# A Mamba scan and a mixture of experts on one core: the end of the scan, the pairs' preparation, the scatters and the shared expert emitted in the order of a list schedule

## The chip, the cores and the metric

The program runs on one core of a Trainium2 chip. The metric is device microseconds (us) of one execution. The kernel is written for five engines that run side by side, each through its own queue in order: PE (TensorE, matmuls and transposes), DVE (VectorE), ACT (ScalarE), POOL (GpSimd, which here also issues the scatters) and SP (which issues most transfers). An instruction starts when it is at the head of its queue and what it waits for has arrived.

## The reference

Eight sequences of 512 tokens, 128 wide (in the kernel B = 8, and a sequence is NC = 4 chunks of Q = 128). First an attention-like part, four layers of a Mamba-2 scan, and then a mixture of experts, each inside a layer norm with shift, scale and gate.

```python
mod = (_silu(L0_c) @ L0_wmod).reshape(L0_c.shape[0], 6, 1, -1)
h = _layernorm(x, axis=-1) * (1 + ca) + sa
x = x + ga * _L0_attn_ref(h, ...)        # 4 layers, then a final rms norm
h = _layernorm(x, axis=-1) * (1 + cb) + sb
x = x + gb * _L0_ffn_ref(h, ...)

# one step of the scan, per sequence
hs = hs * dA_t[:, :, None, None] + dtx_t[..., None] * B_t[:, None, None, :]
y = jnp.einsum('bhpn,bn->bhp', hs, C_t)

# the experts
normed = hidden_states * rsqrt(mean(hidden_states ** 2) + 1e-08) * norm_weight
shared = jnp.maximum(normed @ sw1 + sb1, 0.0) @ sw2 + sb2
probs = jax.nn.sigmoid(flat @ router_w.T)
scores, idx = jax.lax.top_k(probs, TOPK)          # 2 of 8 experts for a token
w = scores / (jnp.sum(scores, axis=-1, keepdims=True) + 1e-06)
return shared + routed
```

## The kernel before

**The scan.** A unit is one sequence in one layer, U = 32 of them; an item is one chunk of a unit, NI = 128 of them, item i being chunk i % 4 of unit i // 4. The scan is computed chunk by chunk, with a state carried from chunk to chunk of a sequence. Items 96 to 111 are the last layer of sequences 0 to 3, items 112 to 127 that of sequences 4 to 7. A loop over slots t emits, in a fixed order, pieces of several items: the loads of decay rows of item t + 4 (`decay_rows`), the difference and the mask of the decays of t + 3 on POOL (`decay_diff`, `decay_mask`), their exponential of t + 2 on ACT (`decay_exp`), transposes of t + 2 on PE and their copy on ACT (`transposes`, which ends in the copy), weighing of t + 1 on POOL (`weigh`), the gram matrix of t + 1 on PE (`gram`), the mix of both on DVE (`mix`), the state's products and step (`state_out`, `state_decay` on POOL, `state_next` on DVE), the output of t - 1 (`chunk_out`, `gate`, `square`), its projection at t - 2 (`project_out`, `out_scale`, whose power is on POOL), and the addition to h at t - 3 (`out_add`). Each piece waits for the one before it of its item, and stands in its engine's queue behind the pieces of other items. From item 115 on, decays are worked at half width on POOL and ACT (`whole`). Units are prepared four units ahead (LEAD), so the last preparation is emitted up to slot t = 115, and from t = 112 on (`drain`) only items remain.

**The pairs.** Four sets of two sequences go through `rejoin(g)`: final rms norm (squares on ACT, power F), addition to x, layer norm (statistics on DVE, power L), shift and scale, rms norm (squares, power G), rows for the experts, transposes, router product, choice of two experts and their places (`first_largest`, prefix sums, the product `pos`), and 16 scatters of 128 rows each to the experts' lists in DRAM (`scatter`, `xg`). A set is called sorted when its row numbers `ix` are there. Powers are on POOL for sets 0 and 1 and on DVE, in twelve steps, for sets 2 and 3. `rejoin` is a generator; every slot steps each of them (`step_pairs`, and once more at its end), set g from slot t = 106 + 8 g on. In slots t >= 112 one scatter is emitted in each slot.

**The shared expert** (`shared`) makes for each sequence four products `phs` with the first weights, ReLU copies on ACT, sixteen products `pes` with the second, and a copy of the sum. It is stepped once a slot from t = 112 on, as soon as a sequence is routed.

**Behind the scan** a loop steps the pairs that are left, emits all scatters that are ready, steps the shared expert, and when the last set is counted, the `tables`: which expert and which rows each of the NT = 39 tiles of 256 rows has. Then come the weights of three tiles (`fetch`), their rows from `xg`, which wait for all scatters, and the experts: `turn`, `hidden`, `combine` for each tile, a scatter of the results to `yg`, and at the end two gathers and a sum per sequence.

**What sets the order.** Slots and the loop behind them are in a manual schedule: all engines follow the order in which the source emits. In the loop behind the scan POOL is left out of it, and the framework's scheduler chooses POOL's order. Three PSUM banks (`pbank`) go round among pairs and shared expert.

Of the kernel before, what the change touches and what calls it, by code (L numbers as in the profile page):

```python
# [20 lines left out]
LEAD = 4  # L21

# [14 lines left out]
def adaln_mamba_moe(  # L37
# [262 lines left out]
    hTx, scatters, rowpools, banks, held = {}, [], [frow], [], {}  # L300
    sets = [(b, b + 1) for b in range(0, B, 2)]
    routed = set()
    scratch = scb.rearrange("p b q -> p (b q)")
# [16 lines left out]

    def mean_squares(h, eps, name, on_pool):
        n = h.shape[1]
        ss = small.tile([P, G2], F32, tag="pss", name=f"pss{name}")[:, :n]
        for j in range(n):
            nc.scalar.activation(unread, h[:, j, :], AF.Square, accum_out=ss[:, j : j + 1])  # L325
            if j % NC == NC - 1:
                yield
        v = small.tile([P, G2], F32, tag="pv", name=f"pv{name}")[:, :n]
        nc.vector.tensor_scalar(v, ss, 1.0 / DM, eps, ALU.mult, ALU.add)
        return power(v, name, on_pool)  # L330

    def rejoin(g):


        seqs = sets[g]
        b0, n = seqs[0], len(seqs) * NC
        parts = [slice(i * NC, (i + 1) * NC) for i in range(len(seqs))]
        md = []
# [6 lines left out]
        def both(k):  # L345

            for i, t in enumerate(parts):
                yield t, md[i][:, k, :].unsqueeze(1).to_broadcast([P, NC, DM])

        mine = slice(b0 % 2 * NC, b0 % 2 * NC + n)  # L350
        h, xt = (v[b0 // 2].rearrange("p b s d -> p (b s) d")[:, mine] for v in (hp, xp))
        on_pool = g < 2
        rs = yield from mean_squares(h, 1e-5, f"F{g}", on_pool)
        yield
        for j in range(n):
            nc.scalar.activation(h[:, j, :], h[:, j, :], AF.Copy, scale=rs[:, j : j + 1])
            if j % NC == NC - 1:
                yield
        for t, m in both(0):
            nc.vector.tensor_mul(h[:, t, :], h[:, t, :], m)  # L360
        yield
        nc.vector.tensor_add(xt, xt, h)
        yield
        mv = small.tile([P, G2, 2], F32, tag="pmv", name=f"mvF{g}")[:, :n]
        for i in range(len(seqs)):
            st = small.tile([P, NC, 6], F32, tag="st", name=f"stF{g}_{i}")
            for s in range(NC):
                nc.vector.bn_stats(st[:, s, :], xt[:, i * NC + s, :])
            for s in range(NC):
                nc.vector.bn_aggr(mv[:, i * NC + s, :], st[:, s, :])  # L370
            yield
        v = small.tile([P, G2], F32, tag="pv", name=f"pvL{g}")[:, :n]
        nc.vector.tensor_scalar_add(v, mv[:, :, 1], 1e-5)
        rs = power(v, f"L{g}", on_pool)
        if on_pool:
            yield
        off = small.tile([P, G2], F32, tag="poff", name=f"off{g}")[:, :n]
        nc.vector.scalar_tensor_tensor(off, mv[:, :, 0], -1.0, rs, ALU.mult, ALU.mult)
        yield
        for j in range(n):  # L380
            nc.scalar.activation(
                h[:, j, :], xt[:, j, :], AF.Identity, bias=off[:, j : j + 1], scale=rs[:, j : j + 1]
            )
            if j % NC == NC - 1:
                yield
        for k in (2, 1):
            for t, m in both(k):
                nc.vector.tensor_tensor(h[:, t, :], h[:, t, :], m, ALU.mult if k == 2 else ALU.add)
            yield
        rs = yield from mean_squares(h, 1e-8, f"G{g}", on_pool)  # L390
        yield

        while scatters and scatters[0][0] in held.get(len(rowpools), [])[:-1]:
            yield
        held.setdefault(len(rowpools), []).append(g)
        rows = [rowpools[-1].tile([P, G2, RW], F32, tag=f"row{c}", name=f"row{c}_{g}")[:, :n] for c in range(2)]
        for j in range(n):
            nc.scalar.activation(rows[0][:, j, :DM], h[:, j, :], AF.Copy, scale=rs[:, j : j + 1])  # L398
            if j % NC == NC - 1:
                yield  # L400
        for c in range(2):
            nc.scalar.activation(rows[c][:, :, DM + 1], tok[:, :n], AF.Copy, bias=float(c * T + b0 * L))
        for i, b in enumerate(seqs):
            t = parts[i]
            pt = banks[-1](f"ptF{b}")
            for s in range(NC):
                nc.tensor.transpose(pt[:, s * P : (s + 1) * P], rows[0][:, i * NC + s, :DM], ident)
            nc.vector.tensor_copy(rows[1][:, t, :DM], rows[0][:, t, :DM])
            yield
            hTx[b] = h[:, t, :].rearrange("p s d -> p (s d)")  # L410
            nc.scalar.activation(hTx[b], pt[:, :L], AF.Copy, scale=nw)
        yield
# [9 lines left out]
        routed.update(seqs)  # L422
        yield
# [11 lines left out]
        m = n * E  # L435
        p = t3("prob")
        nc.scalar.activation(p.rearrange("p s e -> p (s e)"), pr[:, :m], AF.Exp, scale=-1.0)
        yield
# [13 lines left out]
        m1, oh1 = first_largest(p, 1)  # L452
        rest = t3("rest")
        nc.vector.scalar_tensor_tensor(rest, oh1, -2.0, p, ALU.mult, ALU.add)
        yield
        m2, oh2 = first_largest(rest, 2)

        mx, before = t3("mx"), t3("before")
        nc.vector.tensor_add(mx, oh1, oh2)
        yield  # L460
        while len(taken) <= g:
            yield

# [8 lines left out]
        before = src  # L472
        pp = banks[-1](f"pos{g}")
        nc.tensor.matmul(pp[:, :m], below, mx.rearrange("p s e -> p (s e)"), start=True, stop=False)
        nc.tensor.matmul(pp[:, :m], ones, before.rearrange("p s e -> p (s e)"), start=False, stop=True)
        taken.append(fp.tile([P, E], F32, name=f"taken{g + 1}"))
        nc.vector.tensor_add(taken[g + 1], before[:, n - 1, :], mx[:, n - 1, :])
# [3 lines left out]
        yield  # L481
# [6 lines left out]
        for c, oh in enumerate((oh1, oh2)):  # L488
            nc.vector.tensor_mul(oh, oh, pos)
            ix = rowpools[-1].tile([P, G2], mybir.dt.uint32, tag=f"ix{c}", name=f"ix{c}_{g}")[:, :n]  # L490
# [3 lines left out]
            for j in range(n):  # L494
                scatters.append((g, xg, rows[c][:, j, :], ix[:, j : j + 1], "rows"))
        yield
# [15 lines left out]
    xbp = front.enter_context(tc.tile_pool(name="xbp", bufs=5, side="right"))  # L512
# [15 lines left out]
    accs, w12, late = {}, [], []  # L528

    def evacuate(fn, n):  # L530

        if fn is not None:
            late.append(fn)
        while len(late) > n:
            late.pop(0)()

    def shared():

        hds = {}

        def relu(hd, k, ph):
            nc.scalar.activation(hd[:, k, :], ph[:, :L], AF.Relu, bias=b1[:, E, k : k + 1])  # L542

        def keep(b, pe):
            accs[b] = hp[b // 2][:, b % 2]
            nc.scalar.copy(accs[b].rearrange("p s d -> p (s d)"), pe)

        def second(b):
            hd = hds.pop(b)
            pe = pbank(f"pes{b}")  # L550
            for s in range(NC):
                for k in range(FK):
                    nc.tensor.matmul(  # L553
                        pe[:, s * DM : (s + 1) * DM],
# [5 lines left out]
                if s % 2 and s < NC - 1:  # L560
                    yield
            evacuate(lambda: keep(b, pe), 2)
            yield

        for b in range(B):
            while b not in routed:
                if hds:
                    evacuate(None, 0)
                    yield from second(b - 1)
                else:  # L570
                    yield
            hds[b] = hd = xbp.tile([P, NX, L], F32, tag="xbc", name=f"hds{b}")
            for k in range(FK):
                ph = pbank(f"phs{b}_{k}")
                nc.tensor.matmul(ph[:, :L], w12[0][:, k * P : (k + 1) * P], hTx[b], start=True, stop=True)  # L575
                evacuate(lambda hd=hd, k=k, ph=ph: relu(hd, k, ph), 2)
                yield
            if b - 1 in hds:
                yield from second(b - 1)
        evacuate(None, 0)  # L580
        yield from second(B - 1)
        evacuate(None, 0)

    serving = shared()

    def serve():
        nonlocal serving
        if not step(serving):
            serving = None

    with ExitStack() as actx:
# [18 lines left out]
        ss, rss, hns, last_po = {}, {}, {}, []  # L610
# [182 lines left out]
        def sums_b(g):  # L793
# [13 lines left out]
            if g >= (U - LEAD) // GROUP:  # L807
                ncum[g] = scratch[:, m * (g % 2) : m * (g % 2 + 1)]
# [67 lines left out]
        def transposes(i):  # L876
# [5 lines left out]
            for k in range(w // P):  # L882
                nc.tensor.transpose(pt[:, k * P : (k + 1) * P], xbc[u][:, k, t], ident)
# [543 lines left out]
```

## Time and profile before

| what | us |
|---|---|
| median of 9 runs | 1108.61 (1106.09 to 1110.78) |
| the profiled execution's own time | 1110.51 |
| its span | 1108.8 |
| experts, 940 to 1080: PE busy | 130.3 of 140 |
| last addition to h in the scan ends | at 839.96 |
| first scatter to xg starts | at 782.24 |
| last scatter to xg ends | at 916.66 |

Times in the span are counted from its start. The profile gives for each engine how long it was busy in a stretch, each instruction with its start and length, the idle time before it and what ended that, and the chain of waits followed back from the end. A line number there is one of the kernel before; L500 is the call in `scatter`, L310 and L313 to L318 are `power`, L1015 is the power in `out_scale`, L1023 is `out_add`, L907 is `mix`, L841 and L849 are `decay_diff` and `decay_mask`, L575 is the first product of the shared expert, L1271 the request for an expert's rows.

### The profile page before, as it was taken

To read this page: it belongs to the slowest core of one execution; us is meant where nothing else is said; L and a number is where in the kernel's file an instruction comes from. 1 tells how busy PE (TensorE), PEld (TensorE's weight loads), DVE (VectorE), ACT (ScalarE), POOL (GpSimd) and SP (SyncE) were. 2 spreads that over 40 slices of the span, in tenths; PEclk is the share of its full clock that TensorE was granted. 3 is DMA by queue.
4 is the path that set the end of the run, shared out by engine and by line. 5 is a ranking of instruction groups with operands and counts; after the bars stand their busy time and mean duration, and the time that the engine had idled before them with its cause. 6 is when DMAs were issued, how large, how long until landed. Compare 5 with 4: busy or idle time off the path is not lost. (4 is left out here: it accounts for less than half of the span.)

```text
span 1108.8 us, 21442 instructions
## 1 busy us (share of the span) xinstructions
PE 954.8 (86%) x7130; PEld 728.4 (66%) x7130; DVE 827.7 (75%) x1990; ACT 768.4 (69%) x1725; POOL 828.6 (75%) x841
## 2 busy tenths in 40 slices
PE   4568999999999999999999999867666957999985
PEld 2236677767777767777767776556554746888872
DVE  3667889889999898998989898867474464665653
ACT  4577998889889889889889888797535622333320
POOL 6867889889889999899899898775834463555550
PEclk9777999999999999999999999967867988999997
DMA  5141444546555546444334334243000035777747
GB/s 115 5 145 41 139 150 154 179 143 186 169 177 185 168 137 199 163 149 148 117 100 132 113 125 147 82 143 129 32 18 30 27 109 155 218 216 211 225 141 232
DMA packets 134301, 151.18 MB, mean 136 GB/s; under 512 B 22568, under 2 KB 106696, under 8 KB 134192
## 3 DMA queue, kind: packets, MB, share of 16 engines
q1 hardware_dynamic: 127184, 137.91, 41.3%
q0 software_dynamic: 4672, 9.42, 2.5%
q10 hardware_dynamic: 2336, 2.50, 0.7%
q8 instruction: 56, 0.92, 0.3%
q14 instruction: 53, 0.43, 0.1%
HBM read 120.07 MB, written 29.71 MB: 135 GB/s over the span
## 5 line engine op out<-in xcount | busy, mean ns | idle before, releaser
L698 DVE SCALAR_TENSOR_TENSOR xbc<-px,cw,xbc 128x511 f32<-128x511 f32 (+2 forms) x384 | 286.0, 745 | 30.8 <-ACT xbc L688 23.7
L841 POOL TENSOR_TENSOR dV<-dV,cum 128x1024 f32<-128x1024 f32 (+1 forms) x128 | 231.9, 1812 | 0.0
L907 DVE TENSOR_TENSOR dV<-dV,ptx 128x1024 f32<-128x1024 f32 x128 | 155.2, 1212 | 16.2 <-ACT xT L885 16.2
L849 POOL TENSOR_SCALAR_AFFINE_SELECT dV<-dV 128x1024 f32<-128x1024 f32 x128 | 141.8, 1108 | 9.3
L892 POOL TENSOR_TENSOR xd<-xT,dt 128x512 f32<-128x512 f32 (+1 forms) x128 | 120.6, 943 | 34.6 <-ACT xT L885 34.6
L500 POOL DMA_INDIRECT yg<-y,ix x78 | 84.2, 1079 | 81.0 <-DVE y L1313 66.3
L862 ACT ACTIVATE dV<-dV 128x1024 f32<-128x1024 f32 (+1 forms) x128 | 129.1, 1009 | 14.7 <-POOL dV L849 14.4
L688 ACT ACTIVATE xbc<-px,cbias,cw 128x512 f32<-128x512 f32 x128 | 99.4, 776 | 10.0 <-PE px L677 9.5
L500 POOL DMA_INDIRECT xg<-row,ix x64 | 62.9, 984 | 50.6 <-ACT hds L542 29.3
L677 PE MATMUL px<-hT,Wi 128*128 128x512 f32 x192 | 100.4, 605 | 0.0
L916 PEld LDWEIGHTS py<-xbc,st 128*128 128x128 f32 x384 | 60.8, 201 | 54.7 <-issue 37.2
L991 ACT ACTIVATE sq<-g 128x256 f32<-128x256 f32 x128 | 52.4, 410 | 57.7 <-DVE g L987 43.6
L1295 ACT ACTIVATE hd<-ph,bs 128x256 f32<-128x256 f32 x78 | 32.8, 471 | 84.1 <-PE ph L1289 81.7
L1007 PE MATMUL po<-Wo,g 128*128 128x128 f32 x512 | 89.4, 298 | 0.0
L1003 PEld LDWEIGHTS po<-ones,sq 128*128 128x128 f32 x512 | 68.2, 194 | 31.2 <-issue 21.3
L975 PE MATMUL py<-dV,xd 128*32 128x128 f32 x2048 | 85.6, 287 | 0.0
L965 PEld LDWEIGHTS py<-xbc,dg 128*128 128x128 f32 x512 | 79.0, 201 | 6.8 <-issue 1.0
L1003 PE MATMUL po<-ones,sq 128*128 128x1 f32 x512 | 78.7, 258 | 5.0 <-ACT sq L991 4.6
L965 PE MATMUL py<-xbc,dg 128*128 128x128 f32 x512 | 81.6, 284 | 0.0
L1302 PE MATMUL pe<-w,hd 128*128 128x128 f32 x624 | 75.9, 275 | 0.0
L1289 PE MATMUL ph<-xt,w 128*128 128x256 f32 x312 | 75.7, 387 | 0.1
L1302 PEld LDWEIGHTS pe<-w,hd 128*128 128x128 f32 x624 | 72.7, 192 | 0.1
(249 smaller groups left out, 2259.8 us busy)
## 6 DMA issues: line engine op xcount, KB each, us to landing
dV<-crow SPq DMA_DIRECT2D x128, 512.0 KB
w<-in_L_ffn_ew_dram SPq DMA_DIRECT2D x78, 256.0 KB
xg<-blank SPq DMA_DIRECT2D x64, 260.0 KB
ecum<-crow SPq DMA_DIRECT2D x256, 48.0 KB
rows<-xg SPq DMA_DIRECT2D x39, 130.0 KB
b<-in_L_ffn_eb_dram SPq DMA_DIRECT2D x39, 64.0 KB
x<-in_L_attn_x_dram SPq DMA_DIRECT2D x8, 256.0 KB
md<-mods SPq DMA_DIRECT2D x8, 256.0 KB
```

The source lines that it names most:

```text
L500: i = nc.gpsimd.indirect_dma_start(out=to, out_offset=bass.IndirectOffsetOnAxis(ap=ix, axis=0), in_=of, in_offset=None)
L677: nc.tensor.matmul(px[v, k][:, :L], Wi[l][:, c0 : c0 + P], hT[v], start=True, stop=True)
L688: nc.scalar.activation(xbc[v][:, k, :], px[v, k][:, :L], AF.Identity, bias=cbias[:, l, k : k + 1], scale=cw[:, l, k, KT - 1 : KT],)
L698: nc.vector.scalar_tensor_tensor(xbc[v][:, k, d:], px[v, k][:, : L - d], cw[:, l, k, KT - 1 - d : KT - d], xbc[v][:, k, d:], ALU.mult, ALU ...
L841: nc.gpsimd.tensor_tensor(dV[i][:, :w], dV[i][:, :w], cums[g][:, h0 : h0 + w].unsqueeze(2).to_broadcast([P, w, Q]), ALU.subtract,)
L849: nc.gpsimd.affine_select(out=dV[i], in_=dV[i], pattern=[[0, NH], [1, Q]], compare_op=ALU.is_ge, fill=-1e30, base=0, channel_multiplier=-1,)
L862: nc.scalar.activation(dV[i][:, :w], dV[i][:, :w], AF.Exp)
L892: nc.gpsimd.tensor_mul(xds[i][:, :w], xv.unsqueeze(1).to_broadcast([P, w, NH, HD]), dts[g][:, :w, h0 : h0 + NH].unsqueeze(3).to_broadcast( ...
L907: nc.vector.tensor_mul(Ms[i], Ms[i], pg.pop(i).unsqueeze(1).to_broadcast([P, NH, Q]))
L965: nc.tensor.matmul(py[i][:, k, :], dg[l][:, k, :], xbc[u][:, k, t], start=False, stop=True, skip_group_check=True,)
L1003: nc.tensor.matmul(pp[:, 2 * DM + c : 2 * DM + c + 1], sq[:, k, :], ones[:, 0:1], start=(k == 0), stop=(k == NB - 1))
L1302: nc.tensor.matmul(pe[:, s, :], hd[:, k, s * P : (s + 1) * P], w2[:, k, :], start=(k == 0), stop=(k == FK - 1))
```

## The change

The slot loop now ends before t = 112 (TAIL). What it emitted from there on, and the loop behind it, becomes streams of pieces: each scan engine's lane in the old order of slots (PE, DVE, ACT, POOL), one stream for each `rejoin`, one for the scatters (`send`), two for the shared expert (products and copies) and one for the tables. Each piece names its engine, a cost in us, what it needs, what it gives, and which PSUM bank it takes or drops. `arrange` repeats: of all heads whose needs are given and for which a bank is free, take the one whose start by these costs, plus the stream's lag, is earliest, emit it and book its cost on its engine. PE, DVE, ACT and SP follow this order; for POOL the framework's scheduler chooses from t = 112 on.

The rest: sets 0 and 1 now have their powers on DVE and the first scaling of h on POOL (two instructions a set, in place of eight on ACT); sets 2 and 3 have their powers on POOL. No set is begun before t = 112. Rows of all sets are in one pool of two buffers. `transposes` and its copy are two pieces, as are `out_scale` and its power. The shared weights are loaded after the last use of the old ones by the list. The tables use scratch space, and are emitted within the list. The first fetch is of two tiles with their rows, then of the third.

```diff
     def rejoin(g):
-        seqs = sets[g]
+        seqs, on_pool = sets[g], g >= 2
...
+        done = ("add", (NL - 1) * B * NC + seqs[-1] * NC + NC - 1)
+        yield one("SP", 0.1), ((done, ("mods", g - 2)) if g > 1 else (done,)), None
...
-        on_pool = g < 2
         rs = yield from mean_squares(h, 1e-5, f"F{g}", on_pool)
-        yield
-        for j in range(n):
-            nc.scalar.activation(h[:, j, :], h[:, j, :], AF.Copy, scale=rs[:, j : j + 1])
-            if j % NC == NC - 1:
-                yield
...
+        else:
+            for t in parts:
+                yield one("POOL", 1.15), (), None
+                nc.gpsimd.tensor_mul(h[:, t, :], h[:, t, :], rs[:, t].unsqueeze(2).to_broadcast([P, NC, DM]))
...
+        yield one("POOL" if on_pool else "DVE", 1.7), (), None
         rs = power(v, f"L{g}", on_pool)
-        if on_pool:
-            yield
+        yield one("DVE", 0.2), (), None
         off = small.tile([P, G2], F32, tag="poff", name=f"off{g}")[:, :n]
...
+    def send():
+
+        for g, seqs in enumerate(sets):
+            for k in range(2 * NC * len(seqs)):
+                last = k == 2 * NC * len(seqs) - 1
+                yield one("POOL", 1.27), (("sorted", g),), ("sent", g) if last else None
+                of, row, ix = scatters.pop(0)
+                assert of == g
+                scatter(xg, row, ix, "rows")
...
+    def arrange(streams):
...
+        while True:
+            best = None
+            for h in heads:
...
+                chain, needs, _, take, _ = (*h["next"], None, None)[:5]
+                if any(k in due for k in needs):
+                    continue
+                if take is not None and len(ring) >= 3 and ring[-3] not in dropped:
+                    continue
+                start = max([free.get(chain[0][0], 0.0), h["at"]] + [when.get(k, 0.0) for k in needs])
+                if best is None or start + h["lag"] < best[0]:
+                    best = start + h["lag"], start, h
...
-        for t in range(-NC * LEAD - EARLY, NI + 4):
+        TAIL = NI - NC * LEAD
+        for t in range(-NC * LEAD - EARLY, TAIL):
...
-            for g, seqs in enumerate(sets):
-                if t == NC * (U - B) + NC * (seqs[-1] + 1) + 2:
-                    gens["pairs", g] = rejoin(g)
...
-            if drain and scatters and item(t + 3):
-                scatter(*scatters.pop(0)[1:])
...
-            if drain:
-                step_pairs()
...
-            if drain and routed:
-                serve()
...
+            if item(t + 3):
+                piece(
+                    one("POOL", 2.14),
+                    lambda: (decay_diff(t + 3), decay_mask(t + 3)),
+                    (("dV", t + 3), ("rows", 0) if t + 3 >= (last - 1) * NC else ("exp", t)),
+                    ("diff", t + 3),
+                )
...
+        for t in range(TAIL, NI + 4):
+            tail_slot(t)
+        streams = [(lane(v), 0.0, False, [x[2] for x in v if x[2]]) for v in lanes.values()]
+        for g in range(len(sets)):
+            gives = [("routed", g), ("taken", g + 1), ("sorted", g)]
+            streams.append((rejoin(g), 0.1 * g, True, gives + [("mods", g)]))
+        streams.append((send(), 1.0, False, [("sent", g) for g in range(len(sets))]))
+        streams.append((shared_products(), 1.0, False, [(k, b) for k in ("pe",) for b in range(B)]))
+        streams[-1][3].extend(("ph", b, k) for b in range(B) for k in range(FK))
+        streams.append((shared_copies(), 0.6, False, [("hidden", b) for b in range(B)]))
+        streams.append((tables(), 3.0, True, []))
+        fixed.close()
+        with tc.manual_schedule(engines=ordered):
+            arrange(streams)
...
-    rowpools.append(ctx.enter_context(tc.tile_pool(name="frow2", bufs=2)))
...
-        while tail or serving or scatters or table or not tab:
...
-            if not fetched and "to" in tab:
-                fetched = [fetch(j) for j in range(3)]
...
-        for rest in fetched:
-            rest()
+    with tc.manual_schedule(engines=ordered):
+        for js in ((0, 1), (2,)):
+            for rest in [fetch(j) for j in js]:
+                rest()
         turn(0)
```

## The prediction

> **What bounds the kernel now.** I read the busy time by stretch first (windows of the span; columns: PE, PEld, DVE, ACT, POOL busy with counts, TensorE clock, DMA share, GB/s).
>
> ```profile
> 702.00:840.00 138.00, 98.39 (x716) 77.28 (x715) 88.54 (x265) 84.72 (x273) 91.00 (x93) 0.78 0.25 80
> 840.00:896.00 56.00, 48.14 (x265) 33.98 (x266) 29.73 (x144) 36.58 (x97) 20.66 (x22) 0.88 0.08 27
> 896.00:918.00 22.00, 7.27 (x65) 7.08 (x64) 10.57 (x31) 1.80 (x3) 16.03 (x16) 0.78 0.44 130
> 940.00:1080.00 140.00, 130.26 (x901) 119.25 (x899) 83.94 (x268) 44.21 (x101) 76.37 (x72) 1.00 0.72 204
> ```
>
> From 940 on the experts keep PE 93% busy, and the edit leaves them alone. From 702 (chunk 112) to 918 no engine is full: orders and hand-overs set the time there. Next the chain of waits (start, length, what), for where this part ends:
>
> ```profile
> 839.35 0.61 DVE h L1023 x2
> ...
> 896.06 0.96 POOL xg L500
> ...
> 915.70 2.27 DMA xg<-row,ix
> 917.99 2.12 DMA rows<-xg
> ```
>
> The scan's last addition ends at 839.96; I call that moment T0. Set 3 is sorted at 895.9, its sixteen scatters end at 916.7, and the first rows of an expert are asked for at 917.99. That request is the quantity to predict: before, it is T0 + 78.0. POOL's timeline shows why:
>
> ```profile
> 782.24 1.14 POOL L500 DMA_INDIRECT xg<-row,ix  x1 [1.24 <-DVE oh L489]
> ...
> 845.90 0.96 POOL L500 DMA_INDIRECT xg<-row,ix  x1 [0.30 <-issue]
> 872.21 0.95 POOL L500 DMA_INDIRECT xg<-row,ix  x1 [25.36 <-ACT hds L542]
> 873.47 0.96 POOL L500 DMA_INDIRECT xg<-row,ix  x1 [0.31 <-issue]
> ...
> 896.06 0.96 POOL L500 DMA_INDIRECT xg<-row,ix  x1 [3.94 <-ACT hds L542]
> ```
>
> Scatters start 1.264 us apart, so one set costs 20.2. Sets 0 and 1 go out from 782 to 847, most of them while the scan still runs; POOL then stands 25 us for set 2.
>
> **What the change moves.** The order of the built program, engine by engine, shows three things. The scan's instructions stand first everywhere, with few of the pairs' between them. Set 0's turn, sort and scatters, and all shared products, now stand behind the scan's end on PE, DVE and POOL. And POOL's order, which the new list does not fix, reads after the scan: power F2, 16 scatters of set 0, powers L2 and F3, 13 of set 1, power G2, 3 of set 1, power L3, 6 of set 2, power G3, 10 of set 2, 16 of set 3. So I price the scan (T0) and the rest apart.
>
> **The scan's end.** POOL is the fullest queue, so I add it up behind chunk 113's mask. Halves of decays, chunks 115 to 127: 13 x (1.04 + 1.09) = 27.7; chunk 114 whole, 1.90 + 1.09 = 3.0; weighing 12 x 1.05 + 4 x 0.61 = 15.0; state decays 8 x 0.61 = 4.9; eight rates x 0.70 = 5.6; dt 0.3. New on POOL are four scalings of h (sets 0 and 1), which took ACT 1.28 each; no row shows them on POOL. From below stands POOL's 128x256 product, 0.61 (2.4 in all), from above its longest 128x512 row, 1.30 (5.2); taken is the usual 128x512 product of xd, 1.05, so 4.2. Sum 60.7. That mask ended at 695.6; set 0's power F (1.64 at 684.5) now comes later, so the start is 694. In the queue the scaling of set 0 waits about 2.4 for DVE's twelve Newton steps (2.0) behind chunk 113's gate. POOL rows over their median between 702 and 757 (1.58 for 0.61, 1.43 and 2.10 for 1.09) add up to about 4 and I keep that. POOL is through with weighing chunk 127 at 694 + 60.7 + 2.4 + 4 = 761.
>
> But weighing chunk 124 stands behind the decays of 126 and 127, 7.4 before that end, at 753.7, and PE's state product of 124 waits for it, with the gram and turns of the next chunks queued behind. PE needs 3.5 a chunk (0.43 + 0.43 + 0.54 + 0.57 + 0.47 + 0.53 + 0.55 from the rows of chunk 118): four chunks, 14.0. Then gate 0.42, square 0.42, output product 1.0, scale 0.15, power 0.70, addition 0.61 and 0.4 of hand-overs: T0 = 771.5, say 772, 68 earlier than now. Check by pace: the list of mixes gives
>
> ```profile
> 731.88 1.22 DVE L907 TENSOR_TENSOR dV<-dV,ptx 128x1024 f32<-128x1024 f32 x1
> ...
> 753.04 1.21 DVE L907 TENSOR_TENSOR dV<-dV,ptx 128x1024 f32<-128x1024 f32 x1
> ```
>
> four chunks in 21.2, 5.3 each, with pairs between; sixteen at that pace end at 780 and T0 near 786. POOL without its waits gives 761. I take 772, since POOL's sum is made of its own rows; both ends go into the range. SP's queue moves too: the loads of md for sets 0 and 1 stand among the decays' loads, those of sets 2 and 3 and the shared weights behind most of them. The tightest is the decay of 118, asked for behind chunk row 15 at some 710, 4.0 before POOL reads it; 512 KB at the 199 GB/s of the best slice take 2.6, so it costs nothing, and if the cover were gone POOL would stand those 2.6. ACT holds 62 and DVE 57 of work in the same stretch, which POOL's 68 covers; if POOL were faster they would be next.
>
> **From T0 to the rows.** Set 0 first: on DVE behind T0 stand two copies and statistics 2.8, L power 2.2, choice 3.9 (862.53 to 866.41), prefix 1.4, rest 2.3: sorted at T0 + 12.6. Scatters to 32.8, power L2 (1.64) to 34.5. Set 2's offset on DVE and four of its scalings on ACT wait for that power, and set 1's second turn, router product and choice are queued behind them. From there: offset 0.2, ACT 1.55 + 0.60, router product 2.2, first shared product 4.4, second 3.6, positions 0.4, last sums 1.6, hand-overs 0.25: set 1 is sorted at 49.3, with POOL idle for 13. Then 13 scatters, power G2, 3 scatters, power L3: 72.8; the same chain, 0.9 longer by two scalings more: set 2 at 88.5, POOL idle for 16. Six scatters and power G3: 97.8; rows 2.4, turns and copies 5.0, router 2.2 and the rest 6.5: set 3 at 113.9, which covers the ten scatters left. As now, 22.1 more to the rows (895.9 to 917.99): 136. Last, PE forms the tables' count only behind shared products of 11 (0.45 + 3.5 + 3.6 + 3.6), then tables 6.8, loads 2.0, two fetches 4.8 on SP, where only the scatters held rows back before: 1.0 late. Sum T0 + 137, against 78 now. Holding back the third block's weights behind the first rows costs nothing: PE needs them some 12 us later, and a fetch takes 3.2 of SP. If that cover were gone it would cost those 3.2.
>
> The router and shared rows above are cold ones, because PE now stands idle ahead of each set:
>
> ```profile
> 836.00 1.02 PE L575 MATMUL phs<-h,ws 128*128 128x512 f32 x2
> 845.54 2.07 PE L575 MATMUL phs<-h,ws 128*128 128x512 f32 x2 [8.53 <-ACT hds L542]
> 849.41 3.83 PE L575 MATMUL phs<-h,ws 128*128 128x512 f32 x4 [1.79 <-ACT h L546]
> ```
>
> Two matmuls take 2.07 after idling and 1.02 in flow (the granted clock of 702 to 840 is 0.78 on average), about 2.0 lost in each of three sets: all warm, 131; 5 worse, 142. The Trainium skill ("TensorE: Matmul & The Clock Gate", What's actually happening) has the clock halved after about 3.4 us of idling and for the next 3.4 busy; by it three starts lose an estimated 5.1, not 6, and gaps under 3.4 in the scan are free. The trace disagrees on the second: at 725.79 a product took 1.19 for 0.60 after 1.70 idle.
>
> One rule speaks against the whole change: in the Trainium skill ("SBUF — State Buffer", SBUF: two separate sides) DVE's products of two SBUF operands and POOL's instructions lock each other out of a shared port, and the list packs both. If some 55 POOL instructions each lost an estimated 0.3 to it, that would be 16 and T0 788, a loss; the rows above show 4.
>
> So rows at 772 + 137 = 909, 9.0 earlier than 917.99, and nothing behind changes. The profiled execution (1110.5, span 1108.8) becomes 1101.5; the median of nine lies 1.9 below it: **1099.6 us**. The likeliest case's own range: T0 761 to 779 and 131 to 142, some 1083 to 1106.
>
> **Rivals.** *The scatters run through* (4%): were each set sorted when POOL is free, 12.6 + 64 x 1.264 + five powers 8.2 + 1.9 to the rows gives T0 + 104, 33 more gained, 1067. For it: POOL's sum is only that. Against it: the powers stand behind whole sets of scatters in POOL's order. *Nothing moves* (10%): T0 near 781, where 137 eats the whole gain: 1108.6. For it is the present pace of 5.3 per chunk. *Slower* (24%): the alternation behind the scan, where scatters, power, sort and scatters follow one another. It costs 59 whatever the scan does and decides from T0 = 783 on: at the 5.3 pace (T0 786) the rows come at 923, 1114; if the chains also run 5 longer, 1119. For it: today a chunk takes 7.7 on average from 702 to 818. Against it: much of that is POOL waiting for pairs and scatters standing among the chunks, which the new order takes out.
>
> **The numbers.** Some 0.2% (2.2 us) is what runs of this kernel can tell from no change. Forecast 62%, scatters through 4%: faster 0.66; same 0.10; slower 0.24. Range 1086 to 1117, which leaves out the ends of both tails.
>
> **What would show it.** T0 (last addition to h) within 761 to 786; no scatter to xg before it; two idle stretches of POOL of 10 to 17 us between scatters, ended by DVE's last sums of a set, with a power just ahead; 60 us or so of scatters and gaps more behind T0. Wrong if scatters appear in the scan, if the gaps are under 5, or if the chunks' pace stays above 5.5.

## The result, and the profile after

The changed kernel takes 1119.73 us (median of 12 runs, 1116.92 to 1125.40), the kernel before 1109.29 (37 runs, 1106.09 to 1112.47): a ratio of 1.0104, interval 1.0092 to 1.0117, so 1.0% slower. The forecast was 1099.6 and its range ended at 1117. The profiled execution took 1128.6 (span 1126.9), 8.9 above the median; so the places read from it are set beside those of a second profile of the same kernel below.

First the windows of the changed kernel's span (columns as in the prediction: length, busy PE, PEld, DVE, ACT, POOL with counts, TensorE clock, DMA share, GB/s):

```profile
702.00:791.00 89.00, 73.98 (x624) 61.25 (x623) 66.47 (x170) 60.68 (x195) 56.43 (x61) 0.83 0.29 95
791.00:840.00 49.00, 29.98 (x133) 20.45 (x134) 29.34 (x139) 30.36 (x92) 21.07 (x19) 0.72 0.11 33
840.00:909.00 69.00, 45.59 (x220) 32.81 (x219) 24.05 (x107) 30.56 (x87) 37.21 (x36) 0.75 0.10 31
```

The scan's end now takes 89 where it took 138, with PE, DVE and ACT fuller and POOL no fuller than it was. Behind it come 118 us in which no engine is even two thirds busy and PE runs at 0.72 to 0.75 of its clock. Three timelines of the same kernel give the anchors (start, length, engine, what; in brackets the idle time before and what ended it). DVE's has the scan's last addition:

```profile
790.38 0.61 DVE L1135 SCALAR_TENSOR_TENSOR h<-po,rg,h 128x128 f32<-128x128 f32 x2 [0.59 <-POOL rg L1128]
```

POOL's has the first scatter of each set and the powers ahead of the two long waits:

```profile
803.74 1.30 POOL L521 DMA_INDIRECT xg<-row,ix  x1 [0.61 <-DVE ix L503]
...
824.35 1.68 POOL L318 TENSOR_TENSOR pyL<-pvL,mhalf 128x8 f32<-128x8 f32 x1
826.39 1.74 POOL L318 TENSOR_TENSOR pyF<-pvF,mhalf 128x8 f32<-128x8 f32 x1 [0.36 <-DVE pvF L341]
841.28 1.31 POOL L521 DMA_INDIRECT xg<-row,ix  x1 [13.15 <-ACT hds L592]
...
863.65 1.67 POOL L318 TENSOR_TENSOR pyL<-pvL,mhalf 128x8 f32<-128x8 f32 x1
882.08 1.03 POOL L521 DMA_INDIRECT xg<-row,ix  x1 [16.76 <-ACT unread L338]
...
908.58 0.96 POOL L521 DMA_INDIRECT xg<-row,ix  x1 [4.76 <-ACT h L596]
```

And SP's queue has the first request for rows:

```profile
932.22 0.86 SPq L1426 DMA_DIRECT2D rows<-xg  x2
```

T0, the end of the last addition to h, is 790.99 (before: 839.96). No scatter precedes it. Set 0 goes out at T0 + 12.7; power L2 stands behind its sixteen scatters; then POOL idles 13.15, and 16.76 after power L3. Rows are asked for at 932.22, T0 + 141.2 (before: T0 + 78.0). From the rows to the end are 194.7 (before 190.8). So the two spans differ by -49.0 + 63.2 + 3.9 = 18.1: the scan did get shorter, and what the scan no longer does costs more behind it. Of the 18.1, only 10.4 is in the medians.

### The profile page after: what moved, and what is told of

Same layout as the page of the kernel before. It is cut to its first block, busy times and chain, and to the rows that moved or that the text cites. A ratio compares the mean times of both kernels' runs of the same rounds, so it can differ in the third digit from the quotient of the medians.

```text
span 1126.9 us, 21513 instructions
## 1 busy us (share of the span) xinstructions
PE 957.7 (85%) x7130; PEld 731.7 (65%) x7130; DVE 829.0 (74%) x1994; ACT 766.3 (68%) x1709; POOL 831.8 (74%) x845
## 5 line engine op out<-in xcount | busy, mean ns | idle before, releaser
L966 ACT ACTIVATE dV<-dV 128x1024 f32<-128x1024 f32 (+1 forms) x128 | 129.1, 1009 | 10.4 <-POOL dV L953 10.1
L792 ACT ACTIVATE xbc<-px,cbias,cw 128x512 f32<-128x512 f32 x128 | 99.3, 776 | 10.4 <-PE px L781 9.9
L1450 ACT ACTIVATE hd<-ph,wm 128x256 f32<-128x256 f32 x78 | 32.7, 470 | 84.9 <-PE ph L1444 84.9
```

The source lines that it names most:

```text
L966: nc.scalar.activation(dV[i][:, :w], dV[i][:, :w], AF.Exp)
```

## The experiments

They were run beside the kernel before in three comparisons, on chips that the results number 13 (e0 to e3), 2 (e4 to e7) and 8 (e8 to e11). In all three the kernel before took 1127 to 1130, against 1109 in the first comparison, whose chip has no number on record; what differs is in the last section. Only ratios and places counted from T0 are carried over from one comparison to another. Places are read from one profiled execution of each kernel. In the diffs, lines are those of the changed kernel.

**The changed kernel again (e0_again), no edit.**

> The changed kernel once more, to see what of its trace repeats. If the trace is typical: last addition to h (T0) at 788 to 793, first rows asked for at T0 + 139 to 143, POOL idle 13 and 17 between scatters behind a power, time 1117 to 1123. If the profiled execution (9 us above the median) was an odd one, T0 or the experts behind the rows come out 4 to 9 earlier.

Ratio 1.0086 (1.0058 to 1.0114), so the loss repeats. T0 is 786.78, 4 earlier than in the first profile; scatters, powers and idle stretches of 13.84 and 17.10 stand as there, and the last scatter ends at T0 + 138.6 (138.0 there). Rows come only 16 behind that. From the rows to the end are 192.5, against 193.5 for the kernel before in its second profile (e8): the 3.9 of the first pair of profiles does not repeat, so nothing behind the rows needs an explanation.

**The scan without pairs (e4_bare_scan).** Each set waits for the last addition of the scan:

```diff
-        yield one("SP", 0.1), ((done, ("mods", g - 2)) if g > 1 else (done,)), None
+        end = ("add", NL * B * NC - 1)
+        yield one("SP", 0.1), ((done, end, ("mods", g - 2)) if g > 1 else (done, end)), None
```

> No piece of a pair is begun before the scan's last addition to h, so the scan runs alone under the list; the time of the whole is not the point. Theory S (POOL's sum of 56 to 58 without the pairs' four scalings and waits was right for the scan, and it was the pairs' work among it that made T0 late): T0 at 762 to 772. Rival H (the scan's own hand-overs and its decay loads keep a pace over 5 a chunk): T0 at 778 to 788. Behind T0 the first scatter comes at T0 + 45 to 52 by the list's own sum.

T0 is 773.33, 1.3 above the bound of theory S and far from rival H: the scan alone runs at (765.5 - 695.7) / 16 = 4.4 a chunk. The first scatter is at T0 + 46.7, and the whole takes 1155 in its single execution. What POOL waits for says where the pairs come in. Its waits in the changed kernel, first profile, between 704 and T0 (total, times, longest):

```profile
POOL rg L1128 <- DVE rg L1122: 10.5, 4, 5.4
POOL xd L1000 <- ACT xT L993: 8.1, 4, 4.7
POOL h L371 <- DVE pyF L326: 5.9, 2, 4.4
POOL st L1049 <- DVE st L1065: 3.1, 2, 2.6
POOL dV L945 <- DMA dV<-crow: 3.0, 4, 1.1
```

The same for the scan without pairs:

```profile
POOL rg L1129 <- DVE rg L1123: 7.8, 4, 3.8
POOL xd L1001 <- ACT xT L994: 6.2, 5, 1.9
POOL dV L946 <- DMA dV<-crow: 4.9, 3, 4.1
```

With the pairs among it, POOL waits 5.9 for the Newton steps of power F (the twelve small DVE operations that work out a power) and 3.1 for DVE's state step; the scan without pairs has neither wait. For the rates and copies it waits 4.6 more, for decay loads 1.9 less. POOL is not the full queue that the prediction added up; it waits for DVE and ACT in both.

**How DVE comes to be late.** Two powers of the changed kernel, first profile, by DVE's timeline. Power F0, while POOL stands idle (714.5 to 718.9):

```profile
717.01 0.17 DVE L324 TENSOR_TENSOR ptF<-pyF 128x8 f32<-128x8 f32 x1
717.22 0.17 DVE L325 SCALAR_TENSOR_TENSOR ptF<-ptF,pvF 128x8 f32<-128x8 f32 x1
717.42 0.17 DVE L326 SCALAR_TENSOR_TENSOR pyF<-ptF,pyF 128x8 f32<-128x8 f32 x1
```

Power L0, while POOL works without a pause (725.5 to 735.7):

```profile
732.02 0.54 DVE L321 TENSOR_SCALAR ptL<-pvL 128x8 int32<-128x8 int32 x1
732.60 0.96 DVE L322 TENSOR_SCALAR pyL<-ptL 128x8 int32<-128x8 int32 x1
733.59 0.17 DVE L324 TENSOR_TENSOR ptL<-pyL 128x8 f32<-128x8 f32 x1
733.80 0.94 DVE L325 SCALAR_TENSOR_TENSOR ptL<-ptL,pvL 128x8 f32<-128x8 f32 x1
734.77 0.98 DVE L326 SCALAR_TENSOR_TENSOR pyL<-ptL,pyL 128x8 f32<-128x8 f32 x1
...
736.80 0.17 DVE L326 SCALAR_TENSOR_TENSOR pyL<-ptL,pyL 128x8 f32<-128x8 f32 x1
```

POOL at that time:

```profile
731.92 0.61 POOL L1049 TENSOR_TENSOR st<-st,edec 128x256 f32<-128x256 f32 x1
732.49 1.04 POOL L945 TENSOR_TENSOR dV<-dV,cum 128x512 f32<-128x512 f32 x1
733.61 1.11 POOL L953 TENSOR_SCALAR_AFFINE_SELECT dV<-dV 128x1024 f32<-128x1024 f32 x1
734.69 1.04 POOL L1000 TENSOR_TENSOR xd<-xT,dt 128x512 f32<-128x512 f32 x1
```

PE's timeline behind that power:

```profile
738.64 1.20 PE L1024 MATMUL py<-xbc,st 128*128 128x128 f32 x4 [3.38 <-DVE rg L1122]
739.63 1.06 PE L1033 MATMUL py<-xd,xT 128*128 128x256 f32 x2
740.48 1.06 PE L1073 MATMUL py<-xbc,dg 128*128 128x128 f32 x4
...
750.24 0.61 PE L1073 MATMUL py<-xbc,dg 128*128 128x128 f32 x4
```

The eleven operations from L321 on take 2.18 in the first case and 4.95 in the second. All but one of the first five are stretched from 0.17, up to 0.94 to 0.98, about one POOL instruction (1.04). Each of the four ends 0.02 to 0.03 behind the end of a POOL instruction, and the one that kept its 0.17 (at 733.59) began between two of them; from 735.8 on, when POOL has stopped, they are back at 0.17. PE, behind DVE, idles 3.38 and comes back at half speed, 1.06 for 0.61, until 748. DVE's mix (at 745.74) and ACT's copy (at 747.04) follow PE's late transposes, and that is POOL's longest wait for a copy (4.66, up to 747.61). The stretching repeats: L0 took 4.5 to 5.0 in this kernel's second profile and in the kernels e1, e5 and e10 below as well; F1, with one POOL instruction beside it, took 3.06 in both profiles; and G0, which falls where POOL idles, 2.2 in both profiles and in e1 and e5. The Trainium skill ("SBUF — State Buffer", SBUF: two separate sides) says that POOL and DVE's operations with two SBUF inputs or in a two-port mode share a port, and that whichever starts first keeps it for a whole instruction and blocks the other. That fits the ends seen here; which mode the operations with one input ran in, the trace does not show. The prediction had charged this to POOL alone.

**Powers of sets 0 and 1 back on POOL, of 2 and 3 on DVE (e3_powers_as_before).**

```diff
-        seqs, on_pool = sets[g], g >= 2
+        seqs, on_pool = sets[g], g < 2
...
-        if on_pool:
+        if g >= 2:
             for j in range(n):
```

> Powers of sets 0 and 1 on POOL and of sets 2 and 3 on DVE, as in the kernel before; the rest as changed. Theory N (the Newton steps moved onto DVE inside the scan made T0 late: 4.4 and 1.5 of POOL waiting for them, 3.4 of PE and a cold phase behind the stretched ones): T0 at 780 to 786. Rival P (the scan's pace comes from its own hand-overs, whatever the pairs do): T0 at 789 to 793. Behind T0 no power of sets 2 and 3 stands behind scatters, but powers G0, L1, G1 do stand there: by the list the last scatter ends at T0 + 130; by theory A rows at T0 + 130 to 136, time 1100 to 1112.

T0 782.65, as theory N has it, 4.1 earlier than the changed kernel's 786.78 in the same comparison. But the last scatter ends at T0 + 145.0, not 130, rows come at T0 + 161.0, not 130 to 136, and the ratio is 1.0122 (1.0069 to 1.0175). Sets 2 and 3 are now the long ones (idle stretches of 20.20 and 12.26 ahead of them), so what T0 gains is lost behind it.

**POOL in the list's order (e1_list_pool).** Edges without a wait make POOL issue as the list emits (scatters among themselves and the tables' iotas are left free):

```diff
+        for i in nc.cur_bb.bb.instructions[begun:]:
...
+            for k in (*run, other):
+                if k is not None:
+                    tc.add_manual_dep(i, k.name, link, reason="the list's order")
+            other, run = i, []
```

> POOL follows the list too, so powers L2, F3, G2, L3, G3 go between scatters instead of behind whole sets. Theory A (POOL's own order behind the scan holds the sorts up): T0 stays at 791 within 3, no idle stretch of POOL over 8 right behind a power, rows at T0 + 118 to 126 (the list's own costs put the last scatter's end at T0 + 116), time 1098 to 1106. Rival B (the sorts are as long whoever goes first, because PE, DVE and ACT hold them): rows at T0 + 137 or later, time within 4 of the changed kernel's 1119.7.

Its POOL, where the changed kernel has 13.15 of idling:

```profile
815.30 1.67 POOL L318 TENSOR_TENSOR pyL<-pvL,mhalf 128x8 f32<-128x8 f32 x1 [0.65 <-DVE pvL L388]
817.33 1.74 POOL L318 TENSOR_TENSOR pyF<-pvF,mhalf 128x8 f32<-128x8 f32 x1 [0.36 <-DVE pvF L341]
819.25 1.24 POOL L521 DMA_INDIRECT xg<-row,ix  x1 [0.18 <-issue]
832.62 1.25 POOL L521 DMA_INDIRECT xg<-row,ix  x1 [4.53 <-ACT hds L593]
```

Power L2 starts at T0 + 25.1, amid set 0's scatters, in place of T0 + 33.2 behind them, and the wait for set 1 shrinks to 4.53. The last scatter ends at T0 + 126.1, 12.5 sooner than in the changed kernel's second profile; the list's costs had it at T0 + 116. T0 stays (790.2). The ratio is 0.9945 (0.9923 to 0.9967), and the median 14.5 us under the changed kernel's in the same comparison (the profiled spans are only 8.7 apart: T0 is 3.4 later here, and this execution was the slowest of its ten). For the scatters theory A holds, with less than the size forecast, and an idle stretch of 10.46, without a power ahead of it, remains before set 3. For the rows it does not: they come at T0 + 142.1, 16.0 behind the last scatter as in the changed kernel's second profile, not at T0 + 118 to 126. What held them there is the subject of the early tables below.

**All powers on DVE (e2_powers_dve):** `on_pool` is False for all sets, and the first scaling stays where the change put it.

> All powers on DVE, none on POOL; POOL's order is left to the framework as in the changed kernel, so scatters hold up no power. Theory A: same T0 (791), each power 2.0 to 2.2 on DVE, rows at T0 + 118 to 128, time 1100 to 1108. Rival B: the sorts' chains are no shorter, rows at T0 + 137 or later, time 1117 to 1124.

Ratio 1.0124 (1.0081 to 1.0166), last scatter at T0 + 147.8, idle stretches of 20.42, 17.30 and 16.39 without any power behind a scatter: the numbers are rival B's. But it decides little. Ahead of set 2, ACT stood 10.06 and 3.67 for something that the trace does not name, of the kind told of in the last section, and the eleven operations of power L1 took 8.6 in place of some 2.2, each 0.17 long with gaps between them. So this one is inconclusive. The kernel e3, with no power of sets 2 and 3 behind scatters, has its stretches of 20.20 and 12.26 as well. Theory A rests on the kernel with POOL in order alone; with powers on DVE no run shows shorter sorts.

**Tables early (e5_tables_early, e9_tables_only).** The list puts the count pn (L609) behind the shared products of the last two sequences, because its stream has a lag of 3.0. In both, with and without POOL's order:

```diff
-        streams.append((tables(), 3.0, True, []))
+        streams.append((tables(), 0.5, True, []))
```

> POOL in the list's order, and the tables' lag 0.5 in place of 3.0, which puts the count pn ahead of the shared products of the last two sequences on PE (11.6 earlier by the list). If rows then wait for the scatters alone: rows within 4 of the last scatter's landing, 0 to 3 less than the kernel with POOL in order where PE is as quick as in the first profile of the changed kernel, and 9 to 14 less on the chip where the last two copies of the shared sums came 6.7 and 12.3 after the work before them. If PE was not what held the tables there: no change within 2.

> The changed kernel with the tables' lag 0.5 alone; POOL's order is the changed kernel's. If rows were held by the count pn behind the last shared products on this chip (16 between the last scatter and the rows): rows within 4 of the last scatter, 11 to 14 less than the changed kernel, ratio to before about 0.997. If pn's place counts only together with POOL's order, or on a chip like the first one, where rows came 3.3 after the last scatter: 0 to 2 less, ratio about 1.008.

With POOL in order: rows at 917.14, 2.4 behind the last scatter's end (16.0 in the kernel above), ratio 0.9794 (0.9764 to 0.9824). Alone: rows 3.6 behind it, ratio 0.9906 (0.9871 to 0.9942), a larger gain than expected (0.997). In these comparisons pn's place is worth the most of all edits. In the first profile of the changed kernel, the last scatter starts at 927.98; with the 2.27 to its landing that the chain of before shows, rows could have gone at 930.25 and went at 932.22. There it can be worth no more than about 2.

**Three tiles' weights first (e6_fetch_three),** as in the kernel before, on top of the above:

```diff
-        for js in ((0, 1), (2,)):
+        for js in ((0, 1, 2),):
```

> The kernel with early tables, and the weights of three tiles fetched before the first rows, as in the kernel before. Theory W (the third tile's weights, held back behind the first rows, cost the experts about 4): 3 to 4 less than with two, since the tables are now early enough to hide the 3.2 of SP ahead of the rows. Rival: within 1, the experts' start is set by the rows.

Theory W falls: 3.5 slower, not 3 to 4 faster (ratio 0.9824, 0.9794 to 0.9853, which overlaps the interval above), with rows 4.6 behind the last scatter in place of 2.4, since the third fetch stands ahead of them on SP. By these 2.2 holding it back is right; the rest of the 3.5 is within the noise.

**Powers mixed (e7_powers_mixed, e10_mixed_two).** On top of early tables and POOL's order, all powers on POOL but L0; first with three tiles' weights, then with two:

```diff
-        rs = yield from mean_squares(h, 1e-5, f"F{g}", on_pool)
+        rs = yield from mean_squares(h, 1e-5, f"F{g}", True)
...
-        rs = power(v, f"L{g}", on_pool)
+        rs = power(v, f"L{g}", g >= 1)
...
-        rs = yield from mean_squares(h, 1e-8, f"G{g}", on_pool)
+        rs = yield from mean_squares(h, 1e-8, f"G{g}", True)
```

> As the one with three tiles, and all powers on POOL but L0. Set 0's F power stands in POOL's queue for 1.6 in place of a wait of 2.5 to 4.4 for DVE's twelve steps; F1 likewise. By the waits seen: T0 2 to 5 earlier; by the list's costs the last scatter is 1.5 later. Time 0 to 5 less than with the powers of sets 0 and 1 on DVE; if the powers only change places, within 1.5 of it.

> POOL in the list's order, early tables, all powers on POOL but L0, and the weights of two tiles first, as in the changed kernel. By the two steps seen (3.5 for the third tile's weights behind the rows, 2.5 for the powers on POOL): ratio to before 0.975 to 0.979. If the two only overlap: 0.979 to 0.982.

T0 is 781.6 and 781.4, 9 to 10 earlier than with F0, F1 and G0 on DVE (790.5 and 791.9; more than the 2 to 5 expected), and the last scatter 3 later counted from T0. The ratios are 0.9804 (0.9775 to 0.9833; 2.5 us under the kernel with three tiles, as expected, but within the noise) and 0.9759 (0.9735 to 0.9782, as if the two steps added up). The second is the lowest of all, 2.4% under the kernel before; its interval still overlaps that of early tables with POOL's order (0.9794). In the windows of it, up to its T0 and from there to the rows at 911.39, PE's clock is 0.91 in the scan (0.88 in the changed kernel's second profile, 0.95 without pairs):

```profile
702.00:781.40 79.40, 66.42 (x627) 56.18 (x627) 59.13 (x140) 59.87 (x194) 62.34 (x65) 0.91 0.35 110
781.40:911.40 130.00, 88.74 (x422) 60.67 (x421) 60.96 (x255) 63.09 (x184) 77.64 (x72) 0.80 0.15 46
```

**Pairs ahead of the scan in the list (e11_pairs_first),** with POOL's order, early tables and the powers as before the change:

```diff
-            streams.append((rejoin(g), 0.1 * g, True, gives + [("mods", g)]))
+            streams.append((rejoin(g), (-0.3, -0.2, 0.2, 0.3)[g], True, gives + [("mods", g)]))
```

> POOL in order and early tables, and the pairs of sets 0 and 1 put ahead in the list (lags of -0.3 and -0.2, their powers on POOL), so that 16 and more scatters go out before the scan ends, as in the kernel before. By the list's costs T0 comes 40 later than in the changed kernel's list (113 for 73) and the last scatter 7 later (196 for 189): T0 at 815 to 830, rows 5 to 10 later than in the kernel with POOL in order and early tables, ratio 0.984 to 0.989. Rival (what was lost was the place of sets 0 and 1 behind the scan): rows 5 to 20 earlier than there, ratio 0.962 to 0.975.

T0 830.5, just over the span given; the last scatter ends at T0 + 111.9 and the ratio is 1.0072 (1.0044 to 1.0100), worse than either theory. POOL's timeline behind T0:

```profile
857.05 0.96 POOL L521 DMA_INDIRECT xg<-row,ix  x1 [0.30 <-issue]
889.41 0.96 POOL L521 DMA_INDIRECT xg<-row,ix  x1 [31.40 <-ACT row L414]
...
922.10 0.96 POOL L521 DMA_INDIRECT xg<-row,ix  x1 [12.81 <-issue]
```

Only 11 of the 32 scatters of sets 0 and 1 are out by T0 here, not 16 and more; the last of them, at 857.05, ends at T0 + 27.5, where the kernel before has it at T0 + 6.9. Set 2 comes at T0 + 58.9, where that kernel has it at T0 + 32. So this kernel does not bring back the old place of sets 0 and 1, and does not settle what that place alone is worth. It shows that an earlier start bought with a T0 40 later does not pay, and that the other two sets still come one after the other, 32.7 apart (23.9 in the kernel before).

**The kernel before again (e8_before_again), no edit.**

> The kernel before once more, for its trace on this chip (its time was 1127 and 1130 in the last two comparisons, 1109 in the first). If PE is held here as in the kernels run beside it: the last two copies of the shared sums come 6 to 7 and 12 to 13 after the work before them, in place of 3.2 and 3.0, but the rows, which stand behind the scatters only, come T0 + 76 to 82 as before, and most of the 18 lies elsewhere, in a later T0. On a chip like the first: 1107 to 1111, T0 838 to 842, rows T0 + 78.

T0 840.72, as in its first profile; set 3 is sorted at T0 + 69.5 (56.1 there) and rows come at T0 + 95.6 (78.0). So of the 21.1 between its two profiles 17.6 lie between T0 and the rows, not in T0 as I had written. Against it the changed kernel's second profile (chip 13, this one chip 8) has T0 53.9 earlier, T0 to rows 59.0 longer (154.65 against 95.64) and rows to end 1.1 shorter, 4.0 more in all. The medians of the changed kernel's own comparison are 9.6 apart; this execution of the kernel before lies 4.5 above the median there.

## Why the prediction was wrong

**What bounds the kernel before, and what moves:** right. The scan came first everywhere, no scatter precedes T0, and POOL's order has the powers behind whole sets.

**T0 to rows:** right within 4.2. Forecast and first profile, counted from T0: set 0 at 12.6 and 12.7, set 1 at 49.3 and 50.3, set 2 at 88.5 and 91.1, set 3 at 113.9 and 117.6, rows at 137 and 141.2 (154.65 in the second profile, where the count pn came late). The two idle stretches are there, 13.15 and 16.76 for 13 and 16, and the kernel with POOL in order shows that POOL's own order, with powers behind whole sets, makes 12.5 of the 59 to 63 that this part grew by.

**The scan's end: the step that failed.** T0 was put at 772 and came at 786.8 and 791.0, 14.8 and 19.0 later, the larger part of the 20.1 between 1099.6 and 1119.7. The term that failed is POOL's waiting. The sum runs from chunk 113's mask to the weighing of chunk 127; POOL's timeline has both, in the changed kernel (first profile) and then in the scan without pairs:

```profile
692.77 1.09 POOL L953 TENSOR_SCALAR_AFFINE_SELECT dV<-dV 128x1024 f32<-128x1024 f32 x1
...
779.27 0.62 POOL L1000 TENSOR_TENSOR xd<-xT,dt 128x256 f32<-128x256 f32 x1 [1.21 <-ACT xT L993]
```
```profile
693.10 1.10 POOL L954 TENSOR_SCALAR_AFFINE_SELECT dV<-dV 128x1024 f32<-128x1024 f32 x1
...
763.99 0.62 POOL L1001 TENSOR_TENSOR xd<-xT,dt 128x256 f32<-128x256 f32 x1 [1.21 <-ACT xT L994]
```

The rest of the sum came true: the mask ended at 693.9 (forecast 694), POOL was busy for 61.2 between the two (forecast 60.7, and 64.7 with the 4 for long rows), the four scalings in it took 4.1 (4.2), and from the last weighing to T0 11.1 passed (11). But in between POOL stood idle for 24.8, and for 22.1 in the second profile, where the sum had one wait of 2.4. It was through at 779.9 and 775.7, not at 761.

Without pairs POOL stands for 15.1 in the same stretch, so most of the waiting is the scan's own: hand-overs from DVE and ACT, and decay loads. The sum had nothing for it. Without the 6.6 charged for pairs (4.2 and 2.4) it gave 765.4 for the scan alone, 8 less than the 773.3 measured. Decay loads, costed at nothing and bounded by 2.6, made POOL wait 3.0 in the changed kernel and 4.9 in the scan alone, from 704 on.

The pairs add the rest. With them T0 comes 13.5 and 17.7 later than without (11.9 in e9, whose edit acts behind T0), about twice to three times the 6.6, and DVE and ACT were called covered. What the pairs cost runs through these engines: Newton steps on DVE stretched beside POOL, PE idle behind DVE and then at half clock, POOL waiting for both. Taking powers F0, F1 and G0 off DVE gives 9 to 10 of it back (781.6 against 790.5 and 791.9, all with POOL's order and early tables, in one comparison). How much of that is the stretching and how much the waits for twelve steps, no run separates, and the last 8 (781.4 against 773.3) I did not take apart.

**The check by pace was the better number.** It gave T0 near 786 from 5.3 a chunk, and I set it aside because "POOL's sum is made of its own rows". The changed kernel's pace is (781.17 - 695.37) / 16 = 5.4, under the 5.5 that I had named as the sign of a wrong forecast. That sign was set too high, for the result turns before it: with 137 to the rows the whole gain is gone at T0 = 781, and with the 141.2 measured at 776.8.

**The rival that came true** is *Slower*, the alternation behind the scan. It had its place, its price (59; measured 63.2 and 59.0) and its point (783), and the second of its two times, 1114 and 1119 with longer chains, is 0.7 from the result of 1119.7. It was given 24%, because the forecast took POOL for the engine that sets the scan.

**Third block's weights, and pn:** holding back the first cost nothing, as said; it brings the rows forward by 2.2. The second was put at 1.0; in the first profile it is 2.0, by the landing worked out above. In the later comparisons it was 13 (16.0 behind the last scatter, 2.4 to 3.6 with early tables).

**The port rule** was used on the wrong side: 0.3 for each POOL instruction, a figure that no row stood behind, 16 in all. The rows show POOL at its usual lengths and DVE's smallest operations at five times theirs. T0 of 788, worked out in that sentence by it, was nearer than the 772, but for a reason that the runs do not show: POOL's busy time of 61.2 has no such loss in it.

## What to carry to other kernels

A queue's sum sets the end only if that queue hardly waits: before adding up the fullest engine, list what it waits for, and when a pace read from the same trace disagrees by 15 us, the pace has the hand-overs in it. A list schedule knows only the costs that it is given and the queues that follow it; an engine left out of its order (POOL, 12.5 us to the last scatter) and a stream with a careless lag (the tables, some 13 us in the later comparisons) each cost as much as this change lost. Work taken off a critical stretch must go somewhere that is idle *in order*: four sorts behind the scan, each waiting for the last, cost 59 to 63 more for a scan shorter by 49 to 54.

## What the runs showed of the hardware

Small operations of DVE beside a busy POOL can take as long as a POOL instruction each: the eleven of a power took 2.2 with POOL idle, 3.06 with one POOL instruction beside them and 4.5 to 5.0 with POOL working on.

PE at half clock can stay there for long: after 3.38 idle its products took about twice their time from 738.6 to 748, at a granted clock of 0.50 and with PE busy for 9.36 of 9.40:

```profile
738.60:748.00 9.40, 9.36 (x63) 8.21 (x63) 4.52 (x9) 4.48 (x15) 4.07 (x6) 0.50 0.16 58
```

The Trainium skill ("TensorE: Matmul & The Clock Gate", What's actually happening) has it warm again after some 3.4 busy; here it was over 9.

In all three later comparisons, on the chips numbered 13, 2 and 8, the copies of the last shared sums (eight sequences, sixteen products each) come late. ACT in the changed kernel, first profile, and then the same two copies in its second profile:

```profile
914.87 0.58 ACT L596 COPY h<-pes 128x512 f32<-128x512 f32 x1 [2.94 <-PE pes L573]
918.45 0.58 ACT L596 COPY h<-pes 128x512 f32<-128x512 f32 x1 [2.99 <-PE pes L573]
```
```profile
915.59 0.58 ACT L596 COPY h<-pes 128x512 f32<-128x512 f32 x1 [6.76 <-remote]
928.49 0.58 ACT L596 COPY h<-pes 128x512 f32<-128x512 f32 x1 [12.32 <-remote]
```

"remote" marks a releaser that the trace can't name. PE's records show the products issued at the same pace in both up to 915; then the second profile has gaps of 0.48 and 1.03 ahead of the last products and of pn, and none later. DVE's first step behind pn waits 23.2 there, against 10.12 in the first profile, and starts at 928.48, together with the late copy. The same 12.3 stands in all four kernels of that comparison, other kernels have up to 16.5 at one of these two copies, and the kernel before has 17.95 at its last copy. What holds PE, or its results, was not found and not tried. Nor is it shown that the chip is the cause: there are two profiles without such a wait, both from the first comparison, and twelve with it. It is why absolute times of the first comparison and of the experiments are not mixed, and why the gain of early tables, and so the 2.4% of the best kernel, is shown for the later comparisons alone.
